# One queue piece to two steps instead of three, and other step counts per tile, in an attention beside expert tiles

## The chip, the cores and the metric

The kernel runs on one core of a Trainium2 chip. The metric is the time of one launch in microseconds (us) on the device, lower is better; "time" below is the median of several runs. One further execution was recorded by the profiler, and all durations of single instructions come from that one.

## The reference, cut to what matters

Two transformer layers on a batch of 8 sequences of 512 tokens with 256 channels, all in fp32. Each layer is a modulated layer norm, an attention, a gated residual, a second norm, a mixture-of-experts block and another gated residual. Only the second layer's part is touched by the change:

```
h = layernorm(x) * (1 + ca) + sa
x = x + ga * L1_attn(h, w_qkvw, w_out)        # the "second attention"
h = layernorm(x) * (1 + cb) + sb
x = x + gb * L1_ffn(h, Wr, br, W1, W2)

# L1_attn, 16 heads, groups, head size 4:
scores = q @ k^T * scale; attn = softmax(scores); o = attn @ v
return o * w @ w_out
# L1_ffn, 8 experts, one per token:
route = sigmoid(x @ Wr + br); e = argmax(route)
out[token] = max(route) * (gelu(x @ W1[e]) @ W2[e])
```

In this attention the score matrix is a 16 x 16 matrix for every token row and group, with only four products in each sum. It is worked out with element-by-element products and sums on the vector engine and not with matmuls.

## The kernel before, in words

**Expert tiles.** The tokens of some batches are routed, and their rows are scattered (by indirect DMA from GpSimd, L586) to slots sorted by expert. Each run of 128 slots is a tile. A tile loads its rows (L727), transposes them (L733), multiplies with the first weight of its expert (`up`, L760), applies the nonlinearity (L765), multiplies with the second weight (`down`, L775), scales (L782) and scatters its result (L790). In layer 1 a tile is 32 matmuls at L760 and 16 at L775, and it loads four pieces of 512 KB. There are six sets of tiles, `m0` to `m5`: m0 and m1 belong to layer 0, m2 to m5 to layer 1 with two batches each. m2 to m5 run 13 tiles each.

**What runs beside them.** `Line.run` walks the tiles of one set. Its argument `n(j)` says how many steps of another generator are issued with tile j: half of them after the first half of the tile, half after the second, with the fraction carried over in `acc`. A second list, `at`, places single jobs at certain tiles (negative numbers count from the last tile). Beside m1 the first half of the second attention runs (batches 0 to 3, `attend(0, ...)`, 11.5 steps to a tile from tile 3 on), beside m2, m3 and m4 the second half (batches 4 to 7, `attend(1, ...)`, the generator `steps`): 8 steps in tiles 3 to 5 of m2, then 11 steps to a tile in tiles 6 to 12 of m2, 11 in m3, 6 in m4. `until(m4, steps)` at tile 10 of m3 issues steps until m4 has its table; `until(m5, steps)` at tile 10 of m4 does so for m5. `late()` (the output projection of two chunks of the first half, and the routing for m3) is placed into tiles 7 to 11 of m2.

**The attention's own order.** `attend` first normalizes four batches (4 steps), then goes through 16 units, (chunk i of 4) x (gh of 2) x (gc of 2). `project` (L969, matmuls at L978, four steps) makes q, k, v and w for two units. `step(u, v, w)` (L1005) issues the vector instructions of unit u's scores and of the previous unit v's values, with a `yield` after each: 16 steps when both are there, 7 for the first call, 9 for the last. Two of the four score products (`far`, L996) and one of the value products (`farv`, L1031) go to GpSimd; dependencies hold them so that they start when a reduction is next on VectorE. ScalarE does the exponential (L1051).

**The queue behind a chunk.** When a chunk i is done, `finish(i)` is put into the list `behind`. In it come, each piece ended by a `yield`: two empty pieces (not for the last chunk); 16 transposes on TensorE (L1078) with 16 copies on ScalarE (L1083), in two pieces; the output projection (`attend_out`, matmuls L953 and additions into x on VectorE, L957); and then, in the second half, the routing of one batch for m4 (after chunks 0 and 1) or m5 (after chunks 2 and 3). `route` (L482) has five pieces: statistics and norm; transposes, router matmuls (L511) and transposes back; the choice of the expert (L527 to L565, VectorE); a rank matmul (L569, L570); ranks, positions and the scatter (L573 to L586). After chunks 1 and 3 `table` follows. `beside` (L1098) issues a unit's steps and, with some of them, one piece of the queue. What is left over when the units are through is issued piece by piece (L1125).

The program's order gives priorities; the compiler's scheduler then lays out each engine's order, so that instructions of a tile and of a piece stand between each other where both are ready by its model. [...]

Of the kernel before, what the change touches and what calls it, by code (L numbers as in the profile page):

```python
# [28 lines left out]
def kernel(  # L29
# [237 lines left out]
    def drain(steps):  # L267
        for _ in steps:
            pass
# [615 lines left out]
    m2, m3 = Moe(1, even[:2], slots[2]), Moe(1, even[2:], slots[3])  # L885
    m4, m5 = Moe(1, odd[:2], slots[0]), Moe(1, odd[2:], slots[1])
# [8 lines left out]
    line = Line()  # L895
# [63 lines left out]
    def attend(half, owTs, then={}):  # L959
# [136 lines left out]
        behind = []  # L1096

        def beside(main):  # L1098
            for n, _ in enumerate(main):
                yield  # L1100
                if n % 3 == 2 and behind:
                    if next(behind[0], behind) is behind:
                        behind.pop(0)

# [5 lines left out]
        for n in range(len(units) + 1):  # L1110
            u = units[n] if n < len(units) else None
            v = units[n - 1] if n else None
            w = units[n + 1] if n + 1 < len(units) else None
            if v and v[1:] == (0, 0):
                os_[v[0]] = ap1.tile([P, NH1, GW], F32, tag="o", name=f"o{half}_{v[0]}", bufs=2)
            if u and u[1:] == (0, 1) and (half == 1 or 2 * u[0] < HB):
                gate_out(half, u[0])
            if u and u[2] == 0:
                k = 2 * u[0] + u[1] + 1
                if k < 2 * NG:  # L1120
                    yield from project(k // 2, k % 2)
            yield from beside(step(u, v, w))
            if v and v[1:] == (1, NC - 1):
                behind.append(finish(v[0], done[v]))
# [4 lines left out]
    def ready(m):  # L1129
        m.table()  # L1130
        yield
# [3 lines left out]
    def fetch_all(m):  # L1135
        return lambda: [m.fetch_results(i, bufs) for i in range(len(m.batches))]
# [10 lines left out]
    def none():  # L1147
# [13 lines left out]
    steps = attend(1, {}, {  # L1161
        0: [lambda: m4.route(0)],
        1: [lambda: m4.route(1), lambda: ready(m4)],
        2: [lambda: m5.route(0)],
        3: [lambda: m5.route(1), lambda: ready(m5)],
    })

    def until(m, steps):

        def f():  # L1170
            while m.tab is None:
                next(steps)
        return f

    def late():

        for i in range(HB // 2, HB):
            gate_out(0, i)
        yield
        for i in range(HB // 2, HB):  # L1180
            attend_out(0, i, owA[i])
            yield
            yield from m3.route(i - HB // 2)
        yield from ready(m3)

    after = late()
    line.run(m2, steps, lambda j: 11 if j > 5 else 0, {
        0: [fetch_all(m1)],
        1: [none, combines(m1, 0)],
        2: [combines(m1, 1), none],  # L1190
# [3 lines left out]
        **{j: [some(after, 2), some(after, 2)] for j in range(7, 11)},  # L1194
        11: [until(m3, after)],
    }, m3, J=m2.J - 2)
    line.run(m3, steps, lambda j: 11, {-3: [until(m4, steps)]}, m4, J=m3.J - 2)
    line.run(m4, steps, lambda j: 6, {-3: [until(m5, steps)]}, m5, J=m4.J - 2)
    drain(steps)
    line.run(m5, iter(()), lambda j: 0, {  # L1200
        1: [none, fetch_all(m2)],
# [7 lines left out]
    def last(m):  # L1209
# [9 lines left out]
    n = nc.values_load(  # L1219
        many[0:1, 0:1], min_val=0, max_val=2, skip_runtime_bounds_check_because="a count of tiles",  # L1220
    )
# [53 lines left out]
```

## Time and profile before

| What | Value |
|---|---|
| Median of 3 runs | 1991.45 us (1987.05 to 2002.29) |
| Profiled execution, its own time | 2008.82 us |
| Its span, first to last instruction | 2007.1 us, 32461 instructions |
| TensorE busy | 1764.3 us (88%) |
| VectorE busy | 1259.4 us (63%) |
| ScalarE / GpSimd busy | 717.4 us (36%) / 589.8 us (29%) |
| Mean granted TensorE clock | 0.932 |

Times inside the profile are microseconds from the start of the span. PE is TensorE's matmuls, PEld its weight loads, DVE VectorE, ACT ScalarE, POOL GpSimd, SP SyncE, which issues the weight loads. A row of the table by stage has the stretch, its length, then for each engine its busy time with the number of instructions in parentheses, the granted TensorE clock, the busy share of the DMA engines and what they moved in GB/s. A row of an engine's timeline has the start, the duration, the engine, the line and operation with the tile written and the tiles read, the count, and in brackets how long the engine had sat idle before it and what ended that.

### The profile page before, as it was taken

What the parts mean: (1) busy time and instruction counts of PE and PEld (TensorE: products, weight loads), DVE (VectorE), ACT (ScalarE), POOL (GpSimd) and SP (SyncE); (2) the same over time, 40 slices, a digit from 0 to 9 for tenths busy, and PEclk for the clock granted to TensorE, in tenths of its full rate; (3) what the DMA queues carried; (4) which work ended last, traced back from release to release, by engine and by line L of the source; (5) the groups of instructions that cost most, each with busy time, mean ns of one, the idle gap of its engine ahead of it and who ended that gap; (6) DMA issues with size and microseconds to landing.
All of it is one profiled execution on the core that took longest, in us unless ns stands there. A gap on an engine that the chain in (4) does not pass through costs nothing.

```text
span 2007.1 us, 32461 instructions
## 1 busy us (share of the span) xinstructions
PE 1764.3 (88%) x11336; PEld 1541.1 (77%) x11336; DVE 1259.4 (63%) x2228; ACT 717.4 (36%) x1372; POOL 589.8 (29%) x564
## 2 busy tenths in 40 slices
PE   6786866989989989989999999998969989799895
PEld 3354436878878878879899898897868878788785
DVE  5786875443443532225999999722599999986200
ACT  5053112321312212216444435532545546355221
POOL 1033132121121121222444533123245464542110
PEclk8797887999999999989999999999989999899898
DMA  7877768899899997886786777888744655579795
GB/s 231 214 221 198 173 170 277 234 310 279 255 289 280 295 312 237 289 312 231 229 277 229 230 236 230 269 284 295 260 138 135 216 176 185 187 246 344 248 348 167
DMA packets 328536, 488.60 MB, mean 243 GB/s; under 512 B 24017, under 2 KB 184049, under 8 KB 327729
## 3 DMA queue, kind: packets, MB, share of 16 engines
q1 hardware_dynamic: 313840, 445.17, 71.9%
q0 software_dynamic: 14528, 41.31, 5.5%
q8 instruction: 92, 1.51, 0.3%
q14 instruction: 76, 0.61, 0.1%
HBM read 446.40 MB, written 45.27 MB: 245 GB/s over the span
## 4 chain that ended last, share of the span: by engine, by line
PE 53%; DVE 24%; DMA 9%; issue 7%; ACT 4%; POOL 2%; SPq 1%; another core or an unknown queue 1%; DVEq 0%; ACTq 0%; POOLq 0%
PE p L760 23%; PE po L775 13%; PE poa L422 3%; PE pv L405 3%; DVE u L411 3%; DMA w<-in_W_dram 3%; PE pqk L978 3%; DVE s L1019 2%; DVE o L1043 2%; DVE g L767 2%; DMA w<-in_w_dram 1%; DVE o L1060 1%; PE pl L511 1%; DVE u L414 1%; DMA ratio<-rows 1%
## 5 line engine op out<-in xcount | busy, mean ns | idle before, releaser
L760 PE MATMUL p<-xT,w 128*128 128x128 f32 x6144 | 770.2, 282 | 29.3 <-DMA w<-in_W_dram 17.9
L760 PEld LDWEIGHTS p<-xT,w 128*128 128x128 f32 x6144 | 750.3, 198 | 43.9 <-issue 18.0
L775 PE MATMUL po<-w_d,g 128*128 128x256 f32 x1952 | 483.3, 388 | 33.1 <-DVE g L767 22.8
L775 PEld LDWEIGHTS po<-w_d,g 128*128 128x128 f32 x1952 | 357.8, 194 | 87.5 <-DVE g L767 27.9
L790 POOL DMA_INDIRECT ys<-y,to x122 | 151.4, 1241 | 676.8 <-ACT xT L735 413.1
L765 ACT ACTIVATE g<-p 128x512 f32<-128x512 f32 x244 | 145.7, 597 | 482.4 <-PE p L760 411.9
L767 DVE TENSOR_TENSOR g<-g,p 128x512 f32<-128x512 f32 x140 | 95.6, 683 | 293.8 <-PE p L760 238.7
L411 DVE TENSOR_TENSOR_SCAN u<-ratio,pv 128x512 f32<-128x512 f32 x128 | 149.6, 1204 | 54.7 <-PE pv L405 35.5
L405 PE MATMUL pv<-hT,wv_sb 128*128 128x512 f32 x256 | 138.8, 664 | 34.4 <-DVE u L411 27.4
L996 POOL TENSOR_TENSOR far<-q 128x1024 f32<-128x1024 f32 x64 | 133.0, 2079 | 115.8 <-DVE pr L1054 75.7
L422 PE MATMUL poa<-wo_sb,hd 128*128 128x256 f32 x512 | 129.1, 401 | 18.6 <-DVE hd L416 18.3
L782 ACT ACTIVATE y<-po,xs 128x256 f32<-128x256 f32 x122 | 57.7, 473 | 234.4 <-PE po L775 188.1
L422 PEld LDWEIGHTS poa<-wo_sb,hd 128*128 128x128 f32 x512 | 98.7, 199 | 53.6 <-DVE hd L416 32.8
L586 POOL DMA_INDIRECT hs<-ht,pos x96 | 110.2, 1148 | 94.6 <-DVE at L579 32.7
L978 PE MATMUL pqk<-wq_sb,hTa 128*128 128x128 f32 x1024 | 124.2, 280 | 5.3 <-ACT q L985 4.9
L978 PEld LDWEIGHTS pqk<-wq_sb,hTa 128*128 128x128 f32 x1024 | 121.5, 196 | 7.2 <-ACT q L985 5.4
L1031 POOL TENSOR_TENSOR farv<-s,q 128x1024 f32<-128x1024 f32 x32 | 81.6, 2550 | 102.4 <-DVE pr L1028 84.5
L405 PEld LDWEIGHTS pv<-hT,wv_sb 128*128 128x128 f32 x256 | 48.1, 206 | 75.6 <-DVE u L411 34.6
L825 DVE TENSOR_TENSOR yl<-yl,gb 128x512 f32<-128x512 f32 (+1 forms) x24 | 20.6, 865 | 130.9 <-DMA yl<-ys 130.9
L1019 DVE TENSOR_TENSOR s<-s,far 128x1024 f32<-128x1024 f32 x64 | 89.3, 1398 | 0.7 <-POOL far L996 0.7
L414 DVE TENSOR_TENSOR u<-u,factor 128x1024 f32<-128x1024 f32 x64 | 78.1, 1220 | 1.6 <-issue 0.2
L1028 DVE TENSOR_TENSOR pr<-s,q 128x1024 f32<-128x1024 f32 x64 | 77.6, 1215 | 0.1
(205 smaller groups left out, 2003.7 us busy)
## 6 DMA issues: line engine op xcount, KB each, us to landing
w<-in_w_dram SPq DMA_DIRECT2D x280, 512.0 KB
w_d<-in_w_dram SPq DMA_DIRECT2D x140, 512.0 KB
w<-in_W_dram SPq DMA_DIRECT2D x104, 512.0 KB
w_d<-in_W_dram SPq DMA_DIRECT2D x104, 512.0 KB
ratio<-rows SPq DMA_DIRECT2D x128, 256.0 KB
factor<-rows SPq DMA_DIRECT2D x128, 256.0 KB
xs<-hs SPq DMA_DIRECT2D x122, 129.0 KB
yl<-ys POOLq DMA_DIRECT2D x32, 256.0 KB
```

Source lines behind the costliest of these rows:

```text
L405: nc.tensor.matmul(pv, wv_sb[:, k, j * P : (j + 1) * P], hTs[b][:, k, :], start=(k == 0), stop=(k == KD - 1),)
L411: nc.vector.tensor_tensor_scan(out=u[:, i], data0=w[0][:, i], data1=pv, initial=0.0, op0=ALU.mult, op1=ALU.add)
L422: nc.tensor.matmul(po, hds[j][:, t * P : (t + 1) * P], wo_sb[:, j, :], start=(j == 0), stop=(j == NJ - 1),)
L586: ins = nc.gpsimd.indirect_dma_start(out=self.hs, out_offset=bass.IndirectOffsetOnAxis(ap=pos[c][:, t : t + 1], axis=0), in_=ht[c][:, t, : ...
L760: nc.tensor.matmul(p1[:, f * P : (f + 1) * P], ws[n][:, k, f * P : (f + 1) * P], u["xT"][:, k, :], start=(k == 0), stop=(k == KD - 1),)
L765: nc.scalar.activation(gq, pp[0], AF.Silu if l == 0 else AF.Gelu)
L767: nc.vector.tensor_mul(gq, gq, pp[1])
L775: nc.tensor.matmul(u["po"], u["g"][:, q * NF // 2 + f, :], u["w2"][q][:, f, :], start=(q == 0 and f == 0), stop=(q == 1 and f == NF // 2 - 1),
L790: ins = nc.gpsimd.indirect_dma_start(out=self.ys, out_offset=bass.IndirectOffsetOnAxis(ap=to, axis=0), in_=y, in_offset=None,).ins
L978: nc.tensor.matmul(pq[:, hh], hT[:, k, hb * 4 + hh].rearrange("p b r -> p (b r)"), wq_sb[:, k, i, gh].rearrange("p d w g -> p (d w g)"), s ...
L996: ins = nc.gpsimd.tensor_tensor(t, part(u, 0, d, True), part(u, 1, d, False), ALU.mult).ins
L1019: nc.vector.tensor_add(s, s, far[u, d])
```

## The change

It has two parts. In `beside` a piece of the queue goes with every second step and no longer with every third. In the three calls of `line.run` the steps to a tile become 10.5 in m2 (from tile 6), 10.5 in m3 and 7 in m4. No instruction is added or removed; their order is another. `beside` belongs to `attend`, so its edit also touches the first half, beside m1, where the steps to a tile stay at 11.5.

```diff
         def beside(main):
             for n, _ in enumerate(main):
                 yield
-                if n % 3 == 2 and behind:
+                if n % 2 and behind:
                     if next(behind[0], behind) is behind:
                         behind.pop(0)
...
-    line.run(m2, steps, lambda j: 11 if j > 5 else 0, {
+    line.run(m2, steps, lambda j: 10.5 if j > 5 else 0, {
...
-    line.run(m3, steps, lambda j: 11, {-3: [until(m4, steps)]}, m4, J=m3.J - 2)
-    line.run(m4, steps, lambda j: 6, {-3: [until(m5, steps)]}, m5, J=m4.J - 2)
+    line.run(m3, steps, lambda j: 10.5, {-3: [until(m4, steps)]}, m4, J=m3.J - 2)
+    line.run(m4, steps, lambda j: 7, {-3: [until(m5, steps)]}, m5, J=m4.J - 2)
```

## Prediction

> **What bounds the kernel now.** I read the table by stage first, over the stretch in which `steps` runs beside m2, m3 and m4. The cuts are landmarks of ScalarE's timeline: L782 writes a tile's result, so counting 13 back from the end gives m5's tiles, 13 more m4's, and so on. Tile 12 of m2 ends at 1567.5, tile 12 of m3 at 1749.0, tile 9 of m4 at 1846.7.
>
> ```profile
> 1469.00:1510.00 41.00, 31.30 (x174) 27.84 (x175) 37.03 (x78) 19.57 (x31) 19.76 (x15) 0.81 0.49 154
> 1510.00:1567.50 57.50, 50.85 (x360) 47.03 (x359) 54.87 (x89) 30.32 (x47) 28.37 (x22) 0.94 0.57 179
> 1567.50:1610.00 42.50, 40.71 (x289) 37.18 (x289) 40.09 (x54) 26.93 (x52) 21.38 (x15) 1.00 0.53 173
> 1610.00:1655.00 45.00, 38.65 (x257) 35.28 (x255) 44.71 (x52) 21.59 (x35) 28.54 (x14) 0.92 0.58 190
> 1655.00:1700.00 45.00, 42.45 (x297) 40.10 (x298) 42.05 (x56) 27.18 (x51) 21.93 (x14) 0.96 0.58 194
> 1700.00:1749.00 49.00, 35.31 (x215) 31.87 (x214) 49.00 (x82) 18.48 (x29) 21.32 (x13) 0.83 0.57 177
> 1749.00:1831.40 82.40, 76.83 (x508) 69.59 (x507) 71.10 (x99) 43.07 (x84) 38.26 (x30) 0.98 0.83 278
> 1831.40:1880.90 49.50, 41.14 (x229) 36.28 (x229) 19.45 (x68) 21.10 (x45) 7.20 (x8) 0.82 0.79 250
> ```
>
> The third busy figure is VectorE. From 1510 to 1749 it works 230.7 of 239 us, TensorE 208.0. So VectorE sets the pace of m2 and m3 and TensorE has 31 us to spare; in m4's stretch TensorE has 5.6 us to spare. At 1831.4 the last vector instruction of the attention ends. Then comes a chain of latencies (the chain of waits shows them one by one: transposes, projection, routing, table, SyncE's copies, row load, weights) until m5's first tile starts at 1880.9. 49.5 us pass there, in which TensorE works off just three tiles. So the end of the kernel hangs on when VectorE is through, plus a tail.
>
> The rate of VectorE comes from the exponentials, one to a unit:
>
> ```profile
> 1510.54 1.06 ACT L1051 ACTIVATE s<-s 128x1024 f32<-128x1024 f32 x1
> 1809.08 1.06 ACT L1051 ACTIVATE s<-s 128x1024 f32<-128x1024 f32 x1
> ```
>
> 13 units in 298.5 us are 23.0 us each; a unit is 16 steps and two steps of `project`, so 18, and a step takes 1.28 us of VectorE with all that goes with it.
>
> Next I looked at VectorE's own waits, in its timeline: first the two queues behind chunk 1 and 2, then the tail, where the same pieces follow each other with no attention left between them.
>
> ```profile
> 1697.39 0.19 DVE L527 TENSOR_TENSOR z<-pl,br_sb 128x32 f32<-128x32 f32 x1 [2.72 <-PE pl L511]
> 1765.21 0.42 DVE L957 TENSOR_TENSOR x<-x,pao 128x256 f32<-128x256 f32 x1 [3.48 <-PE pao L953]
> 1791.77 0.19 DVE L527 TENSOR_TENSOR z<-pl,br_sb 128x32 f32<-128x32 f32 x1 [1.76 <-PE pl L511]
> ...
> 1828.20 1.23 DVE L825 TENSOR_TENSOR yl<-yl,gb 128x1024 f32<-128x1024 f32 x1 [5.62 <-DMA yl<-ys]
> ...
> 1841.16 0.42 DVE L957 TENSOR_TENSOR x<-x,pao 128x256 f32<-128x256 f32 x1 [2.82 <-PE pao L953]
> 1856.56 0.19 DVE L527 TENSOR_TENSOR z<-pl,br_sb 128x32 f32<-128x32 f32 x1 [6.60 <-PE pl L511]
> ```
>
> The reader is to see that a piece can stop VectorE: it stands in VectorE's order and waits for TensorE. Over the three queues behind chunks 0, 1 and 2 such waits (L957, L527, L553, L573) sum to 11.3 us. In the tail one such chain costs 13.5 us (L957 4.64, L192 1.43, L527 6.60, L553 0.30, L573 0.53). Three chains without any cover would thus cost 40.5 us, and three steps between pieces hide 29.2 of that.
>
> **The steps per tile.** I counted the `yield`s of the generators: 301 steps in all, in both versions. Where each tile starts, before: m3 at step 85, m4 at 236, tile 10 of m4 at 296. After: m3 at 81, m4 at 221, tile 10 of m4 at 291. (At tile 10 of m3 `until(m4)` adds 8 steps before, 4 after, since m4's table comes with step 203 before and 190 after.) So m4 starts 15 steps earlier: 15 x 1.28 = 19 us, at about 1730, if VectorE sets the pace. What VectorE has to do until the last step is the same; the 19 us are only taken out of m2 and m3 and put into m4. TensorE's slack moves with them: 31 - 19 = 12 us left in m2 and m3, 5.6 + 19 = 25 us in m4. Value for the end of the attention: 0. What hides it is that slack; were TensorE unable to fit 208 us of work into 220, m4 would start later than 1730, and its 25 us would absorb up to 19 of it. So the gain of the edit is bounded by VectorE's waits in m4 that come of a crowded TensorE (3.48, 0.17, 1.76, 0.26: 5.7 us), its loss by the same waits in m2 and m3 becoming twice what they are (5.6 us). Value 0, range -5.7 to +5.6.
>
> **The burst.** `until(m5)` issues 10 steps before tile 10's second half instead of 5; the transposes and the projection behind chunk 3 (steps 293 to 295) are now in it and no longer with tile 9. In the trace TensorE does those transposes from 1831.55, after all 32 matmuls of tile 9's first product: just where the burst would put them. The tail's own order (queue left over, one piece a step) is not edited. Value 0; -3 to +3.
>
> **The queue.** After a chunk the pieces come 2 steps apart instead of 3, so a queue of ten takes 20 steps, not 30. Each piece still issues what it issued: 16 transposes (16 x 0.27), 16 ScalarE copies (0.26 each), 8 projection matmuls, the route's some 45 small vector instructions, 4 row-number writes and 4 scatters on GpSimd. No DMA is added; `gate_out` and SyncE's loads are not in the queue. What is queued behind a waiting piece is all of VectorE's attention, and through the exponential ScalarE's gelu of the tiles. The cover per hop falls from 3 steps to 2, 3.4 to 2.3 us at 1.14 us for a product. If cover is in proportion, 29.2 x 1/3 = +9.7 us of waits. It can be 0, since the scheduler lays out VectorE's order and may set a piece's instruction behind more attention (it mingles them singly today), and `project`'s four steps lie between pieces in half of the units without counting. It can be +29.2 if the cover is all lost. A gain is excluded here: a wait does not get shorter by less cover. I take the middle of nothing and the proportion, +5.
>
> **A rule that speaks against it.** GpSimd's products are placed beside reductions. In this trace one slipped:
>
> ```profile
> 1641.27 5.43 DVE L1049 TENSOR_TENSOR s<-s,mx 128x1024 f32<-128x1024 f32 x1
> ```
>
> That instruction usually takes 1.21 us. Just before, two scatters of a route had held GpSimd for 4.48 and 4.22 us, and its two products, late by that, ran at 1641.36 to 1645.6, exactly beside the subtraction. The Trainium skill's page "SBUF — State Buffer", section "Who interferes with whom", says that a VectorE instruction with two SBUF inputs contends with a GpSimd one that reads SBUF, and that the lock is held for the whole instruction. By the rule each of three routes, now packed closer, throws its products out of place: 3 x 4.2 = 12.6 us where 4.2 are paid, +8.4. By the row one route in three was hit, and the pieces of a scatter are one piece in either version: 0. I take the row; +8.4 stays in the range.
>
> **The first half.** VectorE is 100% busy from 950 to 1250 with no wait at any piece, and only chunks 0 and 1 have a projection there, none a route. 0, range -3 to +5; what covers it is that VectorE has other work laid in between at every piece, and without that cover two chains of L957 at 4.64 would cost 9.
>
> **The sum.** 0 + 0 + 5 + 0 + 0 = +5 us. The profiled execution took 2008.82 us (span 2007.1), 17.4 more than the median of the runs; the same 5 us on it give 2014. On the median, 1991.45, it is 1996.
>
> **The rivals.** *Slower: the queue outruns its inputs.* Place: VectorE at L957, L527 and L573 between 1469 and 1831. Price: all cover gone, +29.2, so 2021. It decides once these waits exceed 31 us together (11.3 and 1% of the time). For it: the longest of today's, 3.48, is already as long as the three steps meant to hide it. Against it: L192, 1.43 us in the tail, shows no wait in any of the three queues today. *Faster: VectorE stops waiting.* With 25 us of slack in m4 TensorE is early at each piece there, m4's 5.7 us go, and the combine that was laid ahead of the attention's last two instructions (5.62 us for a load, and 1.2) finds its data: -12.5, 1979. To pass 1% it needs 20 of the some 24 us that VectorE idles from 1445 to 1832. *Nothing happens: the order laid out hardly differs*, 1991.
>
> **How the numbers follow.** I give the small loss (within 1%, own range 1985 to 2009, with no effect in it) 0.53, slower 0.31, faster 0.16, where 1% is about what a measurement of this kernel can tell from no change. The runs of before spread by 15 us. The range 1974 to 2022 takes in the faster case with the other terms' ends and the slower case's price.
>
> **What would show it.** m4's first tile near 1730 and tile 10 of m4 no earlier than now: the pacing as counted. The waits at L957 and L527 before the attention's end: 16 us or so if right, over 31 for the slower case, under 6 for the faster. The time from the attention's last vector instruction to m5's first tile should stay at 49 to 50 us; if that changes by more than 5, the burst was mis-costed. It is wrong if m2 and m3 don't shorten, or if VectorE's waits turn up in the first half.

## The result and the profile after

| | Before | After |
|---|---|---|
| Median time, measured together | 1988.35 us (9 runs) | 2014.52 us (9 runs) |
| Ratio after / before | | 1.012, 95% interval 1.0098 to 1.0142 |
| Profiled execution, its own time | 2008.82 us | 2014.19 us |
| Span | 2007.1 us | 2012.5 us |
| TensorE / VectorE busy | 1764.3 / 1259.4 us | 1766.3 / 1251.3 us |

The changed kernel is 1.2% slower, about 24 us. One of its nine runs, a slow one, took 3568.55 us and is left out of the ratio, which is that of the means of the other runs (2014.3 and 1990.3 us). The predicted 1996 us was 18.5 us short. The two profiled executions cannot be compared by their spans: the one of before lies 20 us above its own median, the one of after lies on its median. So I compare stretches that begin at a common landmark: the result (L782) of tile 5 of m2, at 1447.3 before and at 1432.0 after. Ahead of it the two kernels differ only in the closer queue beside m1, which by itself costs nothing (queue_half0 below).

| Time after that landmark, us | Before | After | Difference |
|---|---|---|---|
| result of m2's tile 12: m3 begins | 120.3 | 125.2 | +4.9 |
| result of m3's tile 12: m4 begins | 301.8 | 307.1 | +5.3 |
| last vector instruction of the attention (L1065) | 383.5 | 372.0 | -11.5 |
| result of m4's tile 8 | 382.1 | 404.2 | +22.1 |
| first transposes behind chunk 3 (L1078) | 384.3 | 411.3 | +27.0 |
| result of m5's tile 0 | 447.9 | 467.1 | +19.2 |
| result of m5's tile 12 | 539.6 | 560.4 | +20.8 |

VectorE is through with the attention earlier, and the end still comes later. The table by stage of the changed kernel shows where (columns as in the prediction; the first busy figure is TensorE):

```profile
1432.00:1899.10 467.10, 395.04 (x2533) 359.08 (x2532) 373.37 (x586) 213.59 (x386) 212.21 (x136) 0.90 0.62 196
1447.30:1557.10 109.80, 84.20 (x536) 77.21 (x535) 103.70 (x177) 54.39 (x81) 53.41 (x38) 0.86 0.49 151
1557.10:1739.00 181.90, 156.51 (x1043) 143.85 (x1042) 174.90 (x241) 86.61 (x158) 97.16 (x55) 0.92 0.57 183
1739.00:1785.00 46.00, 45.25 (x302) 40.78 (x301) 45.49 (x60) 26.99 (x54) 25.17 (x15) 1.00 0.85 283
1785.00:1822.00 37.00, 26.53 (x127) 22.56 (x126) 22.61 (x40) 13.64 (x24) 13.74 (x12) 0.68 0.70 224
1822.00:1886.00 64.00, 54.14 (x331) 47.56 (x330) 12.06 (x62) 24.58 (x56) 9.66 (x10) 0.91 0.73 229
```

The same table of the kernel before, for the whole stretch between the landmarks and for the stretch of m4 that corresponds to the worst one above:

```profile
1447.30:1895.20 447.90, 387.17 (x2533) 353.62 (x2532) 379.22 (x586) 220.02 (x391) 199.56 (x136) 0.92 0.63 204
1787.00:1822.00 35.00, 33.82 (x232) 30.98 (x230) 32.98 (x47) 18.72 (x31) 19.97 (x15) 0.98 0.85 285
```

Between the landmarks TensorE does the same 2533 matmuls. It is busy 395.0 us instead of 387.2 at a lower granted clock (0.90 instead of 0.92), and idle 72.1 us instead of 60.7. So of the 19.2 us, 11.3 are more idle time of TensorE and 7.9 are slower matmuls. The stretch 1785 to 1822 stands out: 127 matmuls in 37 us where there had been 232 in 35, at a clock of 0.68 instead of 0.98.

VectorE's timeline of the changed kernel:

```profile
1625.61 3.76 DVE L1049 TENSOR_TENSOR s<-s,mx 128x1024 f32<-128x1024 f32 x1
1629.75 3.56 DVE L1054 TENSOR_TENSOR pr<-s,q 128x1024 f32<-128x1024 f32 x1
...
1795.96 0.19 DVE L527 TENSOR_TENSOR z<-pl,br_sb 128x32 f32<-128x32 f32 x1 [4.02 <-PE pl L511]
1804.01 0.59 DVE L1065 TENSOR_TENSOR o<-o,q 128x256 f32<-128x256 f32 x1
1849.23 0.42 DVE L957 TENSOR_TENSOR x<-x,pao 128x256 f32<-128x256 f32 x1 [33.81 <-PE pao L953]
```

The last row is the sign that the roles have changed: VectorE ends the attention at 1804.6 and, after a few small instructions of a route, waits 33.81 us for TensorE to come to the last chunk's pieces. The waits that the prediction feared, those at L957, L527, L553 and L573 behind chunks 0 to 2, sum to 11.8 us where they were 11.3.

TensorE's timeline of the changed kernel, its long waits for the attention, and what follows each:

```profile
1540.95 0.66 PE L733 MATMUL pxs<-ident,xs 128*128 128x128 f32 x2 [5.75 <-DMA xs<-hs]
1541.41 9.95 PE L978 MATMUL pqk<-wq_sb,hTa 128*128 128x128 f32 x64
...
1702.09 0.64 PE L570 MATMUL pk<-pre,ones 128*128 128x32 f32 x2 [5.86 <-DVE pre L565]
1724.59 0.66 PE L733 MATMUL pxs<-ident,xs 128*128 128x128 f32 x2 [7.69 <-DMA xs<-hs]
1725.04 3.29 PE L978 MATMUL pqk<-wq_sb,hTa 128*128 128x128 f32 x16
...
1797.51 1.06 PE L519 MATMUL prow<-ident,hTr 128*128 128x128 f32 x4
1804.85 0.61 PE L569 MATMUL pk<-ch,tri 128*128 128x32 f32 x2 [6.28 <-DVE ch L460]
...
1811.57 0.41 PE L570 MATMUL pk<-pre,ones 128*128 128x32 f32 x2 [1.81 <-DVE pre L565]
1812.34 2.85 PE L760 MATMUL p<-xT,w 128*128 128x128 f32 x16
...
1843.26 1.04 PE L1078 MATMUL pot<-ident,o 128*64 128x128 f32 x8
```

The same places before. The rank matmul of the route behind chunk 2 (L569) finds its data, since matmuls of tile 5 of m4 lie between it and the transposes (L519) ahead of it:

```profile
1546.33 5.07 PE L978 MATMUL pqk<-wq_sb,hTa 128*128 128x128 f32 x44
1557.89 0.41 PE L733 MATMUL pxs<-ident,xs 128*128 128x128 f32 x2 [1.25 <-DMA xs<-hs]
...
1792.93 0.60 PE L519 MATMUL prow<-ident,hTr 128*128 128x128 f32 x4
1793.37 0.60 PE L775 MATMUL po<-w_d,g 128*128 128x256 f32 x2
1793.80 0.38 PE L733 MATMUL pxs<-ident,xs 128*128 128x128 f32 x2
1794.64 2.27 PE L760 MATMUL p<-xT,w 128*128 128x128 f32 x18 [0.46 <-ACT xT L735]
1796.76 1.92 PE L775 MATMUL po<-w_d,g 128*128 128x256 f32 x8
1798.52 1.72 PE L760 MATMUL p<-xT,w 128*128 128x128 f32 x14
1800.08 3.62 PE L775 MATMUL po<-w_d,g 128*128 128x256 f32 x16
1803.66 0.38 PE L569 MATMUL pk<-ch,tri 128*128 128x32 f32 x2
```

In the changed order TensorE stands idle 6.28 us for the choice of the expert, then 1.81 us for the counts, with tile matmuls waiting behind it that need neither. On top, the matmuls after the gap are slow: 16 at L760 take 2.85 us at 1812.34, while 14 of them took 1.72 us in the row of before.

### The profile page after: what moved, and what is told of

Same layout as the page of the kernel before. It is cut to its first block, busy times and chain, and to the rows that moved or that the text cites. A ratio compares the mean times of both kernels' runs of the same rounds, so it can differ in the third digit from the quotient of the medians.

```text
span 2012.5 us, 32486 instructions
## 1 busy us (share of the span) xinstructions
PE 1766.3 (88%) x11336; PEld 1544.1 (77%) x11336; DVE 1251.3 (62%) x2228; ACT 711.4 (35%) x1367; POOL 608.8 (30%) x564
## 4 chain that ended last, share of the span: by engine, by line
PE 56%; DVE 20%; DMA 8%; issue 6%; ACT 5%; POOL 3%; SPq 1%; DVEq 0%; ACTq 0%; POOLq 0%
PE p L760 25%; PE po L775 14%; PE pqk L978 4%; PE pv L405 3%; PE poa L422 3%; DVE u L411 3%; DMA w<-in_W_dram 2%; DVE s L1019 2%; DVE o L1043 1%; PE pao L953 1%; DVE g L767 1%; PE pl L511 1%; DMA w<-in_w_dram 1%; DVE o L1060 1%; DMA hs<-hs 1%
## 5 line engine op out<-in xcount | busy, mean ns | idle before, releaser
L760 PE MATMUL p<-xT,w 128*128 128x128 f32 x6144 | 763.1, 281 | 22.5 <-DMA w<-in_W_dram 13.2
L760 PEld LDWEIGHTS p<-xT,w 128*128 128x128 f32 x6144 | 745.5, 197 | 35.5 <-issue 20.5
L775 PE MATMUL po<-w_d,g 128*128 128x256 f32 x1952 | 477.1, 385 | 21.8 <-DVE g L767 16.1
L775 PEld LDWEIGHTS po<-w_d,g 128*128 128x128 f32 x1952 | 355.7, 193 | 72.7 <-DVE g L767 19.3
L422 PE MATMUL poa<-wo_sb,hd 128*128 128x256 f32 x512 | 126.7, 395 | 19.5 <-DVE hd L416 19.2
L782 ACT ACTIVATE y<-po,xs 128x256 f32<-128x256 f32 x122 | 57.7, 473 | 235.8 <-PE po L775 189.7
L978 PE MATMUL pqk<-wq_sb,hTa 128*128 128x128 f32 x1024 | 131.1, 291 | 5.6 <-ACT xT L735 3.0
L978 PEld LDWEIGHTS pqk<-wq_sb,hTa 128*128 128x128 f32 x1024 | 128.4, 207 | 7.6 <-ACT xT L735 3.6
L1031 POOL TENSOR_TENSOR farv<-s,q 128x1024 f32<-128x1024 f32 x32 | 85.7, 2678 | 107.4 <-DVE pr L1028 104.2
L1019 DVE TENSOR_TENSOR s<-s,far 128x1024 f32<-128x1024 f32 x64 | 84.7, 1325 | 0.8 <-POOL far L996 0.7
```

What stands on the lines that cost most here:

```text
L422: nc.tensor.matmul(po, hds[j][:, t * P : (t + 1) * P], wo_sb[:, j, :], start=(j == 0), stop=(j == NJ - 1),)
L760: nc.tensor.matmul(p1[:, f * P : (f + 1) * P], ws[n][:, k, f * P : (f + 1) * P], u["xT"][:, k, :], start=(k == 0), stop=(k == KD - 1),)
L775: nc.tensor.matmul(u["po"], u["g"][:, q * NF // 2 + f, :], u["w2"][q][:, f, :], start=(q == 0 and f == 0), stop=(q == 1 and f == NF // 2 - 1),
L978: nc.tensor.matmul(pq[:, hh], hT[:, k, hb * 4 + hh].rearrange("p b r -> p (b r)"), wq_sb[:, k, i, gh].rearrange("p d w g -> p (d w g)"), s ...
L1019: nc.vector.tensor_add(s, s, far[u, d])
```

## The experiments

Four theories were to be told apart. **A, late pieces:** the last chunk's pieces come too late in TensorE's order, and m5's table with them. **B, pieces too close:** at two steps a piece, TensorE runs into the next link of a route's chain before VectorE has made its input, waits there, and loses clock. **C, steps per tile:** the other counts alone cost the time. **D, projection behind a gate:** with 10.5 steps to a tile, tile 12 of the sets begins ahead of the last `project` in the order, so that 64 matmuls at L978 stand behind the wait for the next set's first rows. The ratios below are against the kernel before on the same chip (where its median was 2010 to 2011 us, not 1988; so ratios are compared, not times), with 95% intervals. Edits are relative to the changed kernel unless said otherwise.

**One part at a time.** The queue's edit alone, the steps' edit alone:

```diff
 queue_only
-    line.run(m2, steps, lambda j: 10.5 if j > 5 else 0, {
+    line.run(m2, steps, lambda j: 11 if j > 5 else 0, {
 (m3 and m4: 11 and 6 in the same way)
 pace_only
-                if n % 2 and behind:
+                if n % 3 == 2 and behind:
```

> The queue's edit alone (a piece with every second step, steps per tile 11, 11 and 6 as before). By the count of steps, tile 10 of m4 starts at step 288 instead of 296, so the last chunk's transposes (step 293) still fall into the burst at tile 10, as in the changed kernel, and the rank matmuls still follow the choice with no tile between. Theory A (the last chunk's pieces come too late in TensorE's order): at least the loss of one tile, +8 us or more. Theory B (TensorE waits at the rank matmul L569 because the pieces are too close, and its clock falls): the whole loss, some +24 us. Theory C (the steps per tile are the cause): 0.

> The steps per tile alone (10.5, 10.5 and 7; a piece with every third step as before). Now the burst for m4's table takes 17 steps, tile 9 of m4 starts at step 297 and the last chunk's transposes (step 293) fall into tile 8, one tile earlier than before. Theory A: not slower, about -7 us. Theory B: 0. Theory C: the loss of the change, some +24 us.

Measured: queue alone 1.0057 (1.0042 to 1.0073), steps alone 0.9998 (0.9987 to 1.0009). C falls: the other counts by themselves cost nothing. The parts don't add up either: 0.57% and 0 against 1.2% together, so the counts cost 0.6% only where the queue is packed.

In the trace of the queue alone one premise of the expectation does not hold: 32 matmuls at L760 do lie between the route's transposes and its rank matmul behind chunk 2, and TensorE waits only 1.61 us there. Nothing is lost up to m4 (it begins at 301.0 after the landmark, before at 301.8); from m4's begin to m5's first result it is 154.3 us where it was 146.1. So the wait at L569 behind chunk 2 is not what the queue alone costs; which wait it is stays open.

In the trace of the steps alone, TensorE waits as long in places as in the changed kernel:

```profile
1558.76 0.66 PE L733 MATMUL pxs<-ident,xs 128*128 128x128 f32 x2 [6.14 <-DMA xs<-hs]
1559.22 9.76 PE L978 MATMUL pqk<-wq_sb,hTa 128*128 128x128 f32 x64
...
1710.04 0.61 PE L569 MATMUL pk<-ch,tri 128*128 128x32 f32 x2 [10.32 <-DVE ch L460]
```

Yet m4 begins at 297.0 there, 4.8 us sooner than before, and m5's first result comes at 444.4 (before 447.9). The first transposes behind chunk 3 come 8.3 us sooner there (376.0) than before, without the gain of 7 us that theory A expected. A long wait is not a loss by itself; it is one where TensorE sets the end.

**The closer queue in the first half alone,** the old one in the second:

```diff
 queue_half0 (with 11, 11 and 6 steps)
-                if n % 2 and behind:
+                if (n % 2 if half == 0 else n % 3 == 2) and behind:
```

> Every second step in the first half of the attention only (beside m1), every third in the second, 11, 11 and 6 as before. All three theories: 0, within 3 us. If it is over +5 us, part of the loss comes from the first half, where none of them looks.

Measured 1.0006 (0.9991 to 1.0022). The first half bears the closer pieces at no cost, as predicted.

**More steps in m4**, so that the attention is issued earlier there:

```diff
 after_m4_8
-    line.run(m4, steps, lambda j: 7, {-3: [until(m5, steps)]}, m5, J=m4.J - 2)
+    line.run(m4, steps, lambda j: 8, {-3: [until(m5, steps)]}, m5, J=m4.J - 2)
```

> The changed kernel with 8 steps to a tile of m4 instead of 7. The attention's last steps then come one tile earlier: the transposes behind chunk 3 (step 293) at the start of tile 9, the table before tile 10. Theory A: 7 to 15 us faster than the changed kernel, so +10 to +18 against before. Theory B: as the changed kernel, +24 us, since the pieces behind chunks 0 to 2 are as close as there. Theory C: slower still than the changed kernel.

Measured 1.0080 (1.0059 to 1.0101). The first transposes behind chunk 3 come at 398.2 instead of 411.3, m5's first result at 461.3 instead of 467.1. It moves two things, though: in its trace the wait at L569 behind chunk 2 is gone too. So it doesn't tell A from B.

**The burst for m5 earlier (A):** by one tile in the kernel with the queue's edit alone, by three tiles in the changed kernel.

```diff
 queue_only_t9: {-3: [until(m5, steps)]}  becomes  {-4: [until(m5, steps)]}
 after_t7:      {-3: [until(m5, steps)]}  becomes  {-6: [until(m5, steps)]}
```

> As queue_only, but the burst for m5's table stands at tile 9 of m4 instead of tile 10; nothing else in the order of the tiles before it changes. queue_only was 11 us slower than before; there VectorE had ended the attention 14 us before TensorE came to the last chunk's transposes. Theory A (TensorE comes to the last chunk's pieces too late): one tile, 7 us, is won back, so about +4 us against before. Theory B (pieces too close, TensorE waits at the rank matmul): nothing changes there, +11 us.

> The changed kernel with the burst at tile 7 of m4 instead of tile 10. In the changed kernel VectorE had ended the attention 39 us before TensorE came to the last chunk's transposes, which is about five tiles, so at tile 7 the inputs are there. Theory A: three tiles of 7.3 us earlier, 15 to 22 us faster than the changed kernel, so +4 to +9 us against before. Theory B: no more than 3 us faster than the changed kernel, so +21 or more.

Measured 1.0035 (1.0015 to 1.0055) against 1.0057, and 1.0095 (1.0068 to 1.0121) against 1.012. The pieces did come earlier: in VectorE's timeline of after_t7 the wait for them is a third of what it was.

```profile
1841.30 0.42 DVE L957 TENSOR_TENSOR x<-x,pao 128x256 f32<-128x256 f32 x1 [11.64 <-PE pao L953]
```

The first transposes behind chunk 3 stand 29 us earlier than in the changed kernel (382.3 against 411.3), and m5's first result comes at 467.0 against 467.1, its last at 558.3 against 560.4. Twenty-nine us earlier for a piece that VectorE visibly waits for, and hardly anything at the end; 0.25% over the runs, within the intervals. TensorE's timeline shows how little a late table can cost. Where m5's first rows and first weights are waited for, before:

```profile
1877.80 0.66 PE L733 MATMUL pxs<-ident,xs 128*128 128x128 f32 x2 [2.99 <-DMA xs<-hs]
1880.89 5.25 PE L760 MATMUL p<-xT,w 128*128 128x128 f32 x32 [2.43 <-DMA w<-in_W_dram]
```

and in the changed kernel:

```profile
1880.88 0.41 PE L733 MATMUL pxs<-ident,xs 128*128 128x128 f32 x2 [3.31 <-DMA xs<-hs]
1884.33 5.71 PE L760 MATMUL p<-xT,w 128*128 128x128 f32 x32 [3.04 <-DMA w<-in_W_dram]
```

These waits are 6.4 us in all where they were 5.4, so the change added some 1 us to them; ahead of them TensorE is still at work on m4's tiles. A, which I thought the likeliest at that point, is at most a small part.

**A gap in the route behind chunk 2 (B).** Three empty pieces are put ahead of the rank matmul of that one route; what follows in this queue comes three pieces later.

```diff
+    def apart(pieces):
+        for n, _ in enumerate(pieces):
+            yield
+            if n == 2:
+                yield
+                yield
+                yield
...
-        2: [lambda: m5.route(0)],
+        2: [lambda: apart(m5.route(0))],
```

> The changed kernel with three empty pieces between the choice and the rank matmul of the route behind chunk 2 (m5's first batch) alone. In the order laid out, one tile's first and second product then stand between prow and pk, as in the kernel before, where the changed kernel has nothing between. Theory A: no change, some +24 us. Theory B: TensorE's wait of 6.3 us at L569 and the low clock of that stretch (0.64 and 0.70) go, 8 to 14 us faster than the changed kernel, so +10 to +16 us against before.

> Both edits on the changed kernel: three empty pieces ahead of that one rank matmul, and the burst at tile 7. If A and B each hold a part and they add up: 24 us or more faster than the changed kernel, so no slower than before, and perhaps the fastest of all. If only A or only B holds: no faster than the better of the two single edits.

Measured: after_apart 1.0080 (1.0060 to 1.0099) against 1.012; with the burst earlier as well, after_apart_t7, 1.0061 (1.0041 to 1.0082) against 1.0095. Both edits together are some 12 us faster than the changed kernel, not the 24 us expected if A and B were the whole loss. TensorE's timeline of after_apart at that place:

```profile
1811.73 0.60 PE L519 MATMUL prow<-ident,hTr 128*128 128x128 f32 x4
1812.19 0.44 PE L733 MATMUL pxs<-ident,xs 128*128 128x128 f32 x2
1814.48 3.84 PE L760 MATMUL p<-xT,w 128*128 128x128 f32 x32 [1.85 <-ACT xT L735]
1818.16 1.46 PE L775 MATMUL po<-w_d,g 128*128 128x256 f32 x6
1819.46 0.38 PE L569 MATMUL pk<-ch,tri 128*128 128x32 f32 x2
```

Tile matmuls are again laid between the transposes and the rank matmul, which finds its data, and 32 matmuls at L760 take 3.84 us, 0.12 each. The next link still waits (L570, 3.56 us where it was 1.81). In that profile m5's first result comes at 461.4, 5.7 us sooner. Laying these three pieces apart, and with them the wait for `ch`, is shown to be worth 7 to 8 us of the 24; with the burst at tile 7 and with the fill below the same edit gives as much again.

**The gate (D).** Five steps are put into tile 12 of m2 and ten into the last tile of m3, so that the last `project` stands ahead of the next set's first rows; m3 and m4 get 10 and 6.1 steps to make up for it. Then the same with the gap:

```diff
 after_fill (and after_fill_apart: with `apart` as above)
+        12: [some(steps, 5)],
...
-    line.run(m3, steps, lambda j: 10.5, {-3: [until(m4, steps)]}, m4, J=m3.J - 2)
-    line.run(m4, steps, lambda j: 7, {-3: [until(m5, steps)]}, m5, J=m4.J - 2)
+    line.run(m3, steps, lambda j: 10, {-3: [until(m4, steps)], -1: [some(steps, 10)]}, m4, J=m3.J - 2)
+    line.run(m4, steps, lambda j: 6.1, {-3: [until(m5, steps)]}, m5, J=m4.J - 2)
```

> The changed kernel with the two late q, k, v, w projections put ahead of the next set's first rows: 5 steps issued at tile 12 of m2 and 10 at tile 12 of m3, ahead of the row load; m3 goes at 10 steps to a tile and m4 at 6.1, so that tile 10 of m3 and tile 10 of m4 start at the same steps as in the changed kernel (186 and 291). Theory D (where 5.75 and 7.69 us of waiting for the first rows of m3 and of m4 stand in the changed kernel, TensorE has lost its 64 projection matmuls to the far side of the wait): 11 to 16 us faster than the changed kernel, so +8 to +13 us against before. Theory A (the last chunk's pieces too late): no change, since their place is the same. Theory B (closer pieces, the wait at the rank matmul): no change.

> The edit of after_fill and that of after_apart (three empty pieces ahead of the rank matmul behind chunk 2) together. If B and D are separate parts of the loss, they add up: some 20 us faster than the changed kernel, so 0 to +6 us against before. If they are one and the same, no better than after_fill.

Measured: after_fill 1.0085 (1.0066 to 1.0104), after_fill_apart 1.0050 (1.0032 to 1.0067). Against the kernels without the fill (1.012 and 1.0080) that is 0.35 and 0.30%, some 6 to 7 us where I had expected 11 to 16; both edits together are 10 us slower than before where I had expected 0 to 6. m3 begins at 119.7, as before the change and 5.5 us sooner than in the changed kernel; but m4 begins at 306.3 against 307.1, so nearly all of it is lost again in m3, at a wait that the changed kernel doesn't have there, and the wait behind chunk 2 is still there. TensorE's timeline of after_fill:

```profile
1605.17 2.17 PE L506 MATMUL ptr<-ident,ht 128*128 128x128 f32 x8 [9.88 <-ACT ht L205]
...
1809.85 0.64 PE L569 MATMUL pk<-ch,tri 128*128 128x32 f32 x2 [7.46 <-DVE ch L460]
```

With the gap added, the same edit as in the other two pairs is worth 0.35% again. In the profiles the fill brings m5's first result only 2.2 us sooner, with the gap 0.5 us, and the counts of m3 and m4 were changed along with it. So what the fill is worth is measured over the runs; that the gate is the reason is not shown.

**11 steps in m2 only**, once with the old queue (pace_m2_11), once with the new (after_m2_11):

```diff
-    line.run(m2, steps, lambda j: 10.5 if j > 5 else 0, {
+    line.run(m2, steps, lambda j: 11 if j > 5 else 0, {
```

> A piece with every third step as before; 11 steps to a tile in m2, 10.5 in m3 and 7 in m4. pace_only (10.5 in m2) was equal to before, with 5.7 us lost in m2 and won in m3. Theory D: at 11 the projection stands ahead of m3's first rows again, the 5.7 us come back, so -4 to -8 us against before, faster than both kernels. Without D: 0.

> The changed kernel with 11 steps to a tile in m2 alone. Theory D: m3 starts 5 us earlier, +19 us against before and not +24. Theories A and B: no change, +24 us.

Measured 1.0015 (1.0003 to 1.0027) and 1.0118 (1.0097 to 1.0140). The first I had hoped to be faster than before; it is not. In both, the 5 us of m2 are won back (m3 begins at 120.9 and 120.0), so the half step less in m2 is shown to cost that set 5 us. In both, the gain is gone before m5. With the new queue it is lost in the very next set, at a wait that the changed kernel doesn't have there (TensorE's timeline of after_m2_11):

```profile
1606.50 2.17 PE L506 MATMUL ptr<-ident,ht 128*128 128x128 f32 x8 [10.51 <-ACT ht L205]
```

It is TensorE standing ahead of a route's transposes while the norm is still being worked out.

**What the runs settle.**

| Edit | Pairs | Worth |
|---|---|---|
| B, gap behind chunk 2 | 1.0120 to 1.0080, 1.0095 to 1.0061, 1.0085 to 1.0050 | 0.34 to 0.40%, 7 to 8 us |
| D, projection ahead of the gate | 1.0120 to 1.0085, 1.0080 to 1.0050 | 0.30 to 0.35%, 6 to 7 us |
| A, burst earlier | 1.0120 to 1.0095, 1.0080 to 1.0061, 1.0057 to 1.0035 | 0.19 to 0.25%, 4 to 5 us, each within its intervals |
| C, other counts, old queue | 0.9998 | 0 |

The second pair of B, the third of B and the second of A were measured on one chip each; the others, both of D's among them, cross chips. A difference of two ratios is uncertain by some 0.3% (both intervals taken together): those of B and D lie at this limit or just beyond it, those of A within it. 0.40, 0.35 and 0.25 add to 1.0 of the 1.2%. All three edits together were not tried, so that they add is taken from the two pairs that were (1.0061 and 1.0050 measured, 1.0055 and 1.0045 by adding). The remaining 0.2%, some 4 us, and the share of A stay open, and so does why the counts cost something only where the queue is packed. No version was faster than the kernel before.

## Why the prediction was right and wrong

The range, 1974 to 2022, holds 2014.5. The likeliest case, a small loss within 1%, did not come: it is slower by just over 1%, to which I gave 0.31. The sign was right, but the mechanism was not: by the profile the loss is in another place than either the likeliest case or the slower rival put it. That the range held is luck in part, since its upper end was the price of that rival.

- **What bounds the kernel: the failed step.** "The end of the kernel hangs on when VectorE is through, plus a tail." VectorE was through 11.5 us sooner after the common landmark, and m5's first result came 19.2 us later. In m4, TensorE's order bounds. Busy shares over m2 and m3 (VectorE 97%, TensorE 87%) had pointed to VectorE, and I called the rest of TensorE "31 us to spare". TensorE's waits by line show what they were, here for the kernel before from 1510 to 1749 (columns: total us, times, longest):

```profile
PE pk L569 <- DVE ch L460: 8.1, 3, 4.6
PE p L760 <- DMA w<-in_W_dram: 5.7, 4, 3.2
PE pk L570 <- DVE pre L565: 5.2, 2, 3.0
PE p L760 <- ACT xT L735: 3.8, 4, 1.9
PE ptr L506 <- ACT ht L205: 2.7, 3, 1.9
PE po L775 <- ACT g L765: 2.4, 1, 2.4
```

  These six rows alone are 27.9 of the 31 us: waits for links of the routes' chains (L569, L570, L506: 16.0), for weights and for the tiles' own links. Idle time is not a reserve where the work that could use it stands behind the waiting instruction, as the tiles' matmuls do behind L569. The same view of the changed kernel from 1495 to 1739 begins with

```profile
PE pxs L733 <- DMA xs<-hs: 13.4, 2, 7.7
PE pk L570 <- DVE pre L565: 10.2, 3, 5.9
```

  so the idle time did not shrink by the 19 us that were to be taken out of it (it is 35 us of 244); it went to other places, the first rows (1.3 us before) in front.
- **Steps per tile, taken at 0 "because the slack hides it".** Alone it is 0 (0.9998). But m4 did not begin 19 us sooner at 1730; after the landmark it began 5.3 us later. My clause for that case, that m4's 25 us of slack "would absorb up to 19 of it", failed as well: with the packed queue the counts cost 0.6%. Half a step less in m2 cost that set 5 us, where the 64 matmuls now stand behind the wait for the first rows (5.75 us), which I had not priced. I had counted in which step each tile begins, but not which matmuls change places with its first rows.
- **The burst, taken at 0 with 3 us either way.** The transposes behind chunk 3 do come with tile 10, but the reading that this is "just where" they stood was off by one tile: 96 of m4's matmuls at L760 were still to come behind them before, 64 in the changed kernel. And m4's tiles were later too, so the transposes came 27 us later after the landmark. From the attention's last vector instruction to m5's first tile 80 us passed, not 49 to 50. By the sign that I had set, the burst was then mis-costed; the edits that move it say 4 to 5 us, within their intervals, since the 80 us are long mostly because VectorE was through early and the tiles' matmuls were late.
- **The queue, +5 (0 to 29.2).** Alone it costs 0.57%, 11.5 us: inside the bounds, twice the value. The place was wrong. I priced "VectorE's waits" and expected 16 us of them; they are 11.8, hardly changed from 11.3. With both parts of the change, what got too short was the other direction of the same chain: TensorE waiting for VectorE's answer (6.28 us behind chunk 2). With the queue alone that wait is 1.61 us, so its 11.5 us are not explained by it. I had listed what is queued behind the waiting VectorE instruction, and not what is queued behind the waiting TensorE instruction of the same piece, which is all of the tiles' matmuls.
- **The shared port, 0 by the row, +8.4 by the rule.** Right as the row had it: the changed trace has two displaced instructions, 3.76 and 3.56 us where 1.21 is usual, 4.9 us together, where the one before cost 4.2.
- **The first half, 0.** Right: 1.0006 with the closer queue only there.
- **The rivals.** The slower one named 2021 us, near what came, but it decides once VectorE's waits pass 31 us; they are 11.8, so its mechanism is refuted and its nearness is chance. Of the faster one, what it describes largely happened: VectorE was through 11.5 us sooner, where the rival counted 12.5. It brought nothing, for the same reason as above.

## What to carry to other kernels

When pieces of a chain that goes back and forth between two engines are moved closer together, price the wait in both directions, and at each place name what stands behind the waiting instruction on that engine. Before calling an engine's idle time slack, list its waits by place: idle that sits ahead of a few chained instructions cannot take up work that is moved elsewhere, and moving it lets the wait turn up at the next link. When step counts are shifted against tiles, look for the bulk of work that changes sides of a gate (here 64 matmuls and the next set's first rows).

## What the runs showed of the hardware that had not been expected

A wait of TensorE can cost more than its length. After 5.75 and 6.14 us of waiting the 64 matmuls at L978 took 9.95 and 9.76 us; at the 0.115 us of the row of before (44 in 5.07 us) they would have taken 7.4. After 7.69 us, 16 of them took 3.29 us instead of 1.8. So 1.5 to 2.6 us come on top of such a wait. Between the landmarks the matmuls are slower by 7.9 us altogether. The Trainium skill's page "TensorE: Matmul & The Clock Gate", section "What's actually happening", states that an idle window of about 3.4 us puts the clock to half and a busy one brings it back. One such window at half clock would make an estimated 1.7 us lost per wait; the rows agree in order of size, but two of the three lose half as much again. I had counted waits without that supplement.

The length of a wait alone does not tell whether the clock falls. In the route behind chunk 2 the same four matmuls at L775 follow the same wait of 1.47 us, in the changed kernel and in after_apart:

```profile
1789.78 2.08 PE L775 MATMUL po<-w_d,g 128*128 128x256 f32 x4 [1.47 <-ACT g L765]
...
1807.72 1.13 PE L775 MATMUL po<-w_d,g 128*128 128x256 f32 x4 [1.47 <-ACT g L765]
```

In the changed kernel the granted clock is 0.50 from there (1789.7) to the end of the wait at L569 (1804.8), so it had fallen ahead of that wait; in after_apart it is 1.00 (1807.7 to 1814.4). So not all of the slow stretch there follows from the 6.28 us, and what made the clock fall stays open.
